# Biased copies of product 1, the order of t1's block sums, and sums moved between engines in a two-layer graph kernel

## The chip, the cores and the metric

The kernel runs on one core of one Trainium2 chip, in float32. The metric is the time of one execution on the device in microseconds (us). Six runs of the kernel before took 1493.88 to 1495.98 us, with a median of 1494.96.

Engines are named as the profile names them: PE is TensorE (matmuls), PEld its weight loads, DVE is VectorE, ACT is ScalarE, POOL is GpSimd, SP is SyncE, which issues most of the transfers.

## The reference

`x` has 128 batches of 128 nodes and 512 features. Cut to what is computed (`b` has one value per node; `Wq`, `Wk`, `Wv` are 512x512 with 512 biases each):

```
h = max(layernorm(x), 0)                       # layer 0, per batch
A = adj @ h;  C = adj @ h + b
x = x + max over n of relu(A + (C - A))        # one value per node, added to all features
h = max(layernorm(x), 0)                       # layer 1
q, k, v = h @ Wq + bq, h @ Wk + bk, h @ Wv + bv   # 8 heads of 64
w = softmax(q k^T / 8 + mask(adj == 0))
x = x + w v
```

Layer 0 adds the same amount to every feature of a node, which the second layernorm takes away again. So one normalised `h` serves both layers.

## The kernel before, in words

The 128 batches are worked in 32 groups of four. The order of every engine's instructions is the order in which the program writes them (`manual_schedule`); nothing is reordered by a planner. The engines run side by side and wait for one another by semaphores where one needs what another made, or overwrites what another still reads.

**Before a group.** `norm(m)` (line 269) makes the statistics of batch m on DVE, then two tiny operations on POOL (a power, line 289, and a product, line 291); `norm_end(m)` (307) then makes `hn` on ACT and, unless told otherwise, adds the bias of v to `x` on POOL with `add_bv` (312, 128x512). Inside the loop ACT and POOL do the statistics (`norm_act`, 293). `adjacency(m)` (356) is one matmul with a maximum on DVE behind it, both through one PSUM bank. `blocks(m)` (316) transposes `hn` in 32x32 blocks on DVE, and `move(m)` (325) puts the blocks of two batches in place with 16 transfers from SP; the result is `hT`.

**The projections.** `Products` (442) makes q, k or v of a group by a scheme of seven half-size products instead of eight, on sums of quarters of the weights (`s1` to `s4`, `weight_sum`, 424) and of `hT` (`t1` to `t4`, `h_sum`, 373). Products 1 and 6 are plain matmuls (line 481). Products 2, 3, 4, 5 and 7 are made by the same scheme once more, on 128x128 blocks (line 587), each from seven block products: `first` (two of them), `inner` (three), `sixth` and `seventh`. For these, block sums of the quarters of `h` are made on POOL (`h_blocks`, 381, tiles `h`) and block sums of the weights once at the start (`weight_blocks`, 409, four sums of 128x128 for each of five quarters, line 422). `h_blocks(g, k, parts)` has k = 0 to 4 for t4, b22, b21, t1 and t3, and the parts 0 (128x256, read by `first`), 1 (128x128, read by `sixth`, `seventh`) and 2 (128x128, `t[:, 3]`, the last, read by the third matmul of `inner`). `h_blocks(g, 3, (2,))`, the last block sum of t1, is read by inner(5). In the text (3,2) means k = 3, part 2.

Results are collected in a tile `u` with three parts and a tile `t` (T7). Product 1 is copied by ACT to `u[0]` (line 508), and for q and k again to `u[1]` with the second half of the bias (two activations, line 496; for v a plain copy, line 510). Then, in the order of `steps` (699), for product p of group g:

- step 0: what is left of the projection before (`end3`), then p1 (matmuls and the copies)
- step 1: first(5), added by DVE to u[0] (first_to, 639); first(7), copied by ACT to T7 (675, 676); product 6 in between; sixth and seventh of 5 and 7, each followed by its addition; `end6`: u[2] = product 6 + bias + u[0] (`add_pf`, line 521, two instructions; for v one, line 517)
- step 2: first(2), seventh(7), terms7(0): u[0] += T7 on POOL (690, 128x512); for q four `h_blocks` on POOL (`mid`); inner(2), inner(5), first43 (first of 4 and of 3), first_to(4) on DVE (665), inner(7); for v `h_sum` of t3 for the next group on POOL (379); terms7(1): u[1] += T7 on POOL
- step 3: `end7`: u[0] = product 7's bank + bias + u[0] (`add_pf`), `end5` (527)
- steps 4 and 5: sixth and seventh of 2, 4 and 3 with their additions (sixth_to(4) is on DVE, line 665, and adds to u[1] and u[2]), inner of 4 and 3, `end4`, and in the next projection `end3`.

A matmul that adds to a bank waits until the addition that reads this bank is through: seventh(4) for sixth_to(4), sixth(7) for first_to(7), inner(4) for `end7`, inner(3) for `end5`.

**A period of the loop** (line 894) is `apply` of the group before (786), `scores` of this group (756, then exponentials on ACT, 764), v of this group, q and k of the next. A table `todo` puts other work behind each step: the masks on POOL (768, four of them behind steps 2 and 3 of q and four behind step 2 of k), block sums, norms, loads. The masks must be done before `apply` reads the weights. The list of h_blocks behind v's last step is line 945. Group 0's first projections (lines 844 to 893) are made without the block scheme for k, by plain q for q.

Of the kernel before, what the change touches and what calls it, by code (L numbers as in the profile page):

```python
# [45 lines left out]
F32 = mybir.dt.float32  # L46
# [6 lines left out]
P = 128  # L53
G = 4
# [115 lines left out]
def tile_adj_preln_d2(  # L170
# [33 lines left out]
    adjT = const.tile([P, D], F32, name="adjT")  # L204
    live = const.tile([P, D], F32, name="live")
    RS = const.tile([P, B, H], F32, name="RS")
    ones = const.tile([P, 1], F32, name="ones")
    flag = const.tile([1, 1], I32, name="flag")
    V = const.tile([P, G, H, HE], F32, name="v")
# [3 lines left out]
    def fast(ctx):  # L213
# [98 lines left out]
        def add_bv(m):  # L312
            x_m = x_of(m)
            nc.gpsimd.tensor_tensor(x_m, x_m, bv_sb, op=ALU.add)  # L314
# [123 lines left out]
        def weight_sums(eng, n):  # L438
            for k in range(4):
                weight_sum(eng, n, k)  # L440

        class Products:
# [59 lines left out]
                nc.vector.tensor_tensor(to, to, what, op=ALU.add)  # L502

            def p1(self):
                self.a = self.bank(0)
                self.mm(self.a, "a11", "b11", True)
                self.u = U
                nc.scalar.copy(self.u[:, 0], self.a)  # L508
                if self.n == "v":
                    nc.scalar.copy(self.u[:, 1], self.a)  # L510
                else:
                    self.biased(self.u[:, 1], self.a, 1)

            def add_pf(self, out, bank, f):

                if self.n == "v":
                    nc.vector.tensor_tensor(out, bank, self.u[:, 0], op=ALU.add)
                    return
                bias = bq_sb if self.n == "q" else bk_sb
                for r in range(2):  # L520
                    nc.vector.scalar_tensor_tensor(
                        out[:, r], bank[:, r], bias[:, 2 * f + r : 2 * f + r + 1],
                        self.u[:, 0, r], op0=ALU.add, op1=ALU.add,
                    )

            def add(self, out, bank, more):
# [172 lines left out]
        def steps(p, tail, mid, t2, t3, late):  # L699

            t = tail + [lambda: None] * 8
            return [
                [t[0], p.p1],
                [call(p.first, 5, True), call(p.first_to, 5), t[1], call(p.p6a, (0,)),
                 call(p.first, 7, True), call(p.first_to, 7), call(p.p6a, (1, 2)),
                 call(p.sixth, 5), call(p.sixth_to, 5), call(p.sixth, 7), call(p.sixth_to, 7),
                 call(p.p6a, (3,)), call(p.seventh, 5), call(p.seventh_to, 5), p.end6],
                [call(p.first, 2, True), call(p.seventh, 7), call(p.seventh_to, 7), call(p.terms7, 0), mid,
                 call(p.inner, 2), p.end2] + [call(p.inner, 5), call(p.first43)][::-1 if late else 1] +
                [call(p.first_to, 2), call(p.first_to, 4),  # L710
                 call(p.inner, 7), t3, call(p.terms7, 1)],
                [p.end7, p.end5],
                [call(p.sixth, 2), call(p.sixth_to, 2), call(p.sixth, 4), call(p.sixth, 3), call(p.sixth_to, 4)],
                [call(p.inner, 4), call(p.inner, 3), call(p.seventh, 2), call(p.seventh, 4),
                 call(p.seventh, 3), call(p.seventh_to, 2), call(p.seventh_to, 4)] + ([t2, p.end4] if p.n == "v" else [p.end4]),
            ]
# [4 lines left out]
        def call(m, *a):  # L721
            return lambda: m(*a)
# [119 lines left out]
        with tc.manual_schedule():  # L842
# [13 lines left out]
            transposes(3)  # L856
            for m in range(G):
                add_bv(m)
            weight_sums(nc.gpsimd, "v")
            plain_q(0, 0)  # L860
            weight_sums(nc.vector, "k")
            for k in range(4):
# [7 lines left out]
            adjacency(3)  # L870
            plain_q(1, 0)
            blocks(G)
            weight_blocks(nc.vector, "v", (3, 2, 0))
            blocks(G + 1)
            move(G + 1)
            weight_blocks(nc.vector, "v", (1, 4))
            plain_q(1, 1)
            k = Products(0, "k")
            more = {
                0: [(adjacency, G), (norm, G + 2), (norm_end, G + 2)],  # L880
                1: [(norm, G + 3), (norm_end, G + 3), (blocks, G + 2)],
                2: [(adjacency, G + 1)], 3: [(blocks, G + 3), (move, G + 3)],
                4: [(adjacency, G + 2)], 5: [(adjacency, G + 3)],
            }
            for s, p in enumerate((k.p1, k.p6, k.p2, k.p7, k.p5, k.p4, k.p3)):
                p()
                for f, m in more.get(s, ()):
                    f(m)
                if s < 2:
                    add_bv(G + s)  # L890
                elif s < 6:
                    weight_sum(nc.gpsimd, "q", s - 2)
            weight_blocks(nc.gpsimd, "q", (3, 2))
            for g in range(NG):
                b = g * G
                if g > 0:
                    apply(g - 1)
                scores(g)
                part, tail = [], []
                for p in [Products(g, "v")] + [Products(g + 1, n) for n in "qk" if g + 1 < NG]:  # L900
                    if p.n == "v" and g in (0, NG - 1):
                        part += [
                            [p.p1], [p.p6], [p.p2], [p.p7], [p.p5], [p.p4, p.p3],
                        ]
                        continue
                    t2 = t3 = mid = lambda: None
                    if p.n == "v":
                        t2 = lambda: h_sum(g + 1, 2)
                        t3 = lambda: h_sum(g + 1, 0, nc.gpsimd)
                    if p.n == "q":  # L910
                        mid = lambda: [
                            h_blocks(g + 1, k, (i,)) for k, i in ((0, 1), (1, 1), (0, 2), (1, 2))
                        ]
                    part += steps(p, tail, mid, t2, t3, g == NG - 2)
                    tail = later(p)
                    if p.n == "k":
                        part[-1] += tail
                        tail = []
                todo = {s: [] for s in range(len(part))}

                def add(s, *what):
                    todo[s].append(what)

                m = b + 2 * G
                if g + 1 < NG:
                    if g > 0:
                        for i in range(G):
                            residual(b - G + i, nc.gpsimd)
                    if m < B:
                        norm(m)  # L930
                        norm(m + 1)
                    else:
                        count(0, b)
                    if 0 < g < NG - 1:
                        add(0, adjacency, m - 1)
                    if g == 0:
                        add(3, h_sum, 1, 0)
                    add(4, h_sum, g + 1, 1)
                    if g == 0:
                        add(4, h_sum, 1, 2)  # L940
                    for k, i in ((4, 0), (4, 1), (3, 0), (3, 1)):
                        add(4, h_blocks, g + 1, k, (i,))
                    add(5, h_blocks, g + 1, 2)
                    add(5, h_sum, g + 1, 3, nc.gpsimd)
                    for k, i in ((0, 0), (1, 0), (3, 2), (4, 2)):
                        add(5, h_blocks, g + 1, k, (i,))
                    if g + 2 < NG:
                        for s, l in next_norms(m).items():
                            for what in l:
                                add(s, *what)  # L950
                    for k, s in enumerate((8, 8, 9, 9, 14, 14, 14, 14)):
                        add(s, mask, nc.gpsimd, b + k // 2, k % 2)
                    if g + 2 < NG:
                        add(0, load, 2 * g + 5)
                    if g + 3 < NG:
                        add(8, load, 2 * g + 6)
                else:
                    for k, s in enumerate((0, 0, 0, 0, 2, 2, 3, 4)):
                        add(s, mask, nc.vector, b + k // 2, k % 2)
                    for i, s in enumerate((0, 0, 0, 1)):  # L960
                        add(s, residual, b - G + i)
                for i in range(G):
                    add((2, 5, 9, 15)[i] if g + 1 < NG else i + 1, add_c, b + i)
                if g == 0:
                    add(0, weight_blocks, nc.gpsimd, "q", (0, 1, 4))
                    for s, k in ((0, 3), (0, 2), (1, 0), (1, 1), (3, 4)):
                        add(s, weight_blocks, nc.vector, "k", (k,))
                for s, ps_ in enumerate(part):
                    for p in ps_:
                        p()  # L970
                    for f, *args in todo[s]:
                        f(*args)
# [49 lines left out]
```

## Time and profile before

| | |
|---|---|
| median of 6 runs | 1494.96 us (1493.88 to 1495.98) |
| profiled execution, its own time | 1495.62 us |
| its span from first to last instruction | 1493.9 us |
| mean granted TensorE clock | 0.999 |
| PE / PEld / DVE / ACT / POOL busy | 99 / 90 / 79 / 44 / 88% |
| from the start to the first scores | 47.60 us |
| one period of the loop | 45.76 us |

The busy time of PE is the time in which a matmul was under way. A busy PE is not PE at its peak, since matmuls are pipelined: a lost tenth of a microsecond shows best in the weight loads, which in the block products follow each other every 0.11 us as long as nothing holds them. In a row of the timeline stand the start and the length in us, engine, line, operation, the tiles (output <- inputs), the shape, how many instructions were merged into the row, and in brackets the idle time ahead of it with what ended it. Every block product is two weight loads and two matmuls in the trace.

### The profile page before, as it was taken

To read this page: it belongs to the slowest core of one execution; us is meant where nothing else is said; L and a number is where in the kernel's file an instruction comes from. 1 tells how busy PE (TensorE), PEld (TensorE's weight loads), DVE (VectorE), ACT (ScalarE), POOL (GpSimd) and SP (SyncE) were. 2 spreads that over 40 slices of the span, in tenths; PEclk is the share of its full clock that TensorE was granted. 3 is DMA by queue.
4 is the path that set the end of the run, shared out by engine and by line. 5 is a ranking of instruction groups with operands and counts; after the bars stand their busy time and mean duration, and the time that the engine had idled before them with its cause. 6 is when DMAs were issued, how large, how long until landed. Compare 5 with 4: busy or idle time off the path is not lost.

```text
span 1493.9 us, 38616 instructions
## 1 busy us (share of the span) xinstructions
PE 1474.0 (99%) x14565; PEld 1343.4 (90%) x14565; DVE 1186.0 (79%) x2984; ACT 661.9 (44%) x1487; POOL 1318.5 (88%) x1564
## 2 busy tenths in 40 slices
PE   7999999999999999999999999999999999999997
PEld 5899999999999999999999999999999999999997
DVE  7787877778877878778787778887787877778877
ACT  3444454454444444544444444435444444444432
POOL 5989889889899898898898988989989989889882
PEclk9999999999999999999999999999999999999999
DMA  5232222322223312233222233122332222331211
GB/s 168 53 86 42 63 77 77 86 65 46 76 75 84 86 33 72 76 78 86 58 52 76 76 85 86 28 77 75 80 86 56 54 74 76 86 84 28 62 43 59
DMA packets 307836, 105.67 MB, mean 71 GB/s; under 512 B 273152, under 2 KB 273280, under 8 KB 307648
## 3 DMA queue, kind: packets, MB, share of 16 engines
q1 hardware_dynamic: 307328, 102.84, 26.7%
q8 instruction: 117, 1.92, 0.6%
q14 instruction: 71, 0.58, 0.1%
q0 software_dynamic: 176, 0.27, 0.1%
q10 hardware_dynamic: 144, 0.07, 0.0%
HBM read 37.03 MB, written 33.55 MB: 47 GB/s over the span
## 4 chain that ended last, share of the span: by engine, by line
PE 77%; POOL 19%; DVE 2%; issue 1%; DMA 1%; ACT 0%; SPq 0%; DVEq 0%; POOLq 0%
PE bk L587 37%; PE bk L481 17%; POOL h L396 13%; PE bk L786 8%; PE bk L756 8%; PE bk L348 7%; POOL u L690 3%; POOL hs L379 3%; DMA wk_sb<-in_L_gnn_Wk_dram 1%; DVE sk_sb L434 0%; DVE ssv_sb L422 0%; DVE hs L379 0%; POOL xp L314 0%; ACT hn L308 0%; DVE o L804 0%
## 5 line engine op out<-in xcount | busy, mean ns | idle before, releaser
L768 POOL TENSOR_TENSOR w<-w,live 128x512 f32<-128x512 f32 x248 | 308.7, 1279 | 0.0
L690 POOL TENSOR_TENSOR u<-u,t 128x512 f32<-128x512 f32 x184 | 234.5, 1275 | 76.2 <-DVE t L639 53.3
L665 DVE TENSOR_TENSOR u<-u,bk 128x256 f32<-128x256 f32 x552 | 206.2, 414 | 58.5 <-PE bk L587 35.7
L764 ACT ACTIVATE w<-bk 128x512 f32<-128x512 f32 x256 | 128.9, 624 | 271.1 <-PE bk L756 271.1
L639 DVE TENSOR_TENSOR u<-u,bk 128x128 f32<-128x128 f32 x368 | 109.2, 317 | 99.4 <-PE bk L587 96.4
L308 ACT ACTIVATE hn<-xp,nmr,rstd 128x512 f32<-128x512 f32 x124 | 100.5, 810 | 159.2 <-POOL nmr L305 97.3
L816 POOL TENSOR_TENSOR o<-xp,o 128x512 f32<-128x512 f32 x122 | 152.2, 1287 | 20.2 <-DVE RS L803 20.2
L314 POOL TENSOR_TENSOR xp<-xp,bv_sb 128x512 f32<-128x512 f32 x128 | 159.9, 1289 | 3.2 <-ACT hn L308 1.9
L352 DVE TENSOR_REDUCE amax<-bk 128x1 f32<-128x512 f32 x128 | 86.6, 677 | 75.0 <-PE bk L348 75.0
L508 ACT COPY u<-bk 128x512 f32<-128x512 f32 x95 | 55.1, 580 | 183.6 <-PE bk L481 183.6
L348 PE MATMUL bk<-hn,adjT 128*128 128x512 f32 x248 | 127.0, 594 | 0.9 <-DVE amax L352 0.9
L786 PE MATMUL bk<-v,w 128*64 128x65 f32 x4096 | 126.5, 222 | 0.0
L786 PEld LDWEIGHTS bk<-v,w 128*64 128x64 f32 x4096 | 122.0, 138 | 4.1 <-issue 0.3
L756 PE MATMUL bk<-qT,kT 64*128 64x128 f32 x2048 | 122.9, 275 | 0.0
L756 PEld LDWEIGHTS bk<-qT,kT 64*128 64x128 f32 x2048 | 116.8, 188 | 2.5 <-issue 0.3
L587 PE MATMUL bk<-ssv_sb,h 128*128 128x128 f32 x720 | 111.4, 277 | 0.1
L587 PEld LDWEIGHTS bk<-ssv_sb,h 128*128 128x128 f32 x720 | 98.6, 191 | 14.2 <-issue 13.9
L396 POOL TENSOR_TENSOR h<-hT,h 128x128 f32<-128x128 f32 x186 | 96.4, 518 | 7.3
L804 DVE TENSOR_TENSOR o<-bk,RS 128x448 f32<-128x448 f32 (+1 forms) x161 | 93.7, 582 | 5.5
L812 ACT ACTIVATE xp<-xp,c 128x512 f32<-128x512 f32 x128 | 91.2, 715 | 0.0
L587 PEld LDWEIGHTS bk<-h,ssq_sb 128*128 128x128 f32 x558 | 75.8, 191 | 15.3 <-DVE u L665 7.7
L321 DVE STREAM_TRANSPOSE tb<-hn 128x512 f32<-128x512 f32 x124 | 87.1, 703 | 2.2 <-ACT hn L308 2.2
(198 smaller groups left out, 4077.0 us busy)
## 6 DMA issues: line engine op xcount, KB each, us to landing
out_dram<-o SPq DMA_DIRECT2D x128, 256.0 KB, 2.4
xp<-in_x_dram SPq DMA_DIRECT2D x62, 512.0 KB, 5.0
hT<-tb SPq DMA_DIRECT2D x992, 32.0 KB, 1.9
xp<-in_x_dram SPq DMA_DIRECT2D x4, 256.0 KB, 3.9
wq_sb<-in_L_gnn_Wq_dram SPq DMA_DIRECT2D x2, 512.0 KB, 7.8
wk_sb<-in_L_gnn_Wk_dram SPq DMA_DIRECT2D x2, 512.0 KB, 10.0
wv_sb<-in_L_gnn_Wv_dram SPq DMA_DIRECT2D x2, 512.0 KB, 11.0
bv_sb<-in_L_gnn_bv_dram POOLq DMA_DIRECT2D x1, 256.0 KB, 7.8
```

The lines of the kernel that those rows point to most:

```text
L314: nc.gpsimd.tensor_tensor(x_m, x_m, bv_sb, op=ALU.add)
L348: nc.tensor.matmul(PA[m], adjT, HN[m], start=True, stop=True)
L396: nc.gpsimd.tensor_tensor(o, x, y, op=ALU.subtract)
L481: nc.tensor.matmul(bank[:, r, :], lhs, rhs, start=first and i == 0, stop=i == 3, skip_group_check=True,)
L587: nc.tensor.matmul(out, lhs, rhs, start=start, stop=True, skip_group_check=True)
L665: nc.vector.tensor_tensor(to, to, what, op=ALU.add)
L690: nc.gpsimd.tensor_tensor(u, u, T7, op=ALU.add)
L756: nc.tensor.matmul(psc[j][:, f, :], KT[g][r, f, i * D : (i + 1) * D], QT[g][r, f, i * D : (i + 1) * D], start=True, stop=True,)
L764: nc.scalar.activation(w[:, j], psc[j], AF.Exp, scale=HD ** -0.5)
L768: eng.tensor_tensor(w[:, j], w[:, j], live_h, op=ALU.mult)
L786: nc.tensor.matmul(pav[r, c : c + HE], w[:, h % 2, h // 2, r], V[:, i, h, :], start=True, stop=True,)
L816: eng.tensor_tensor(y, x_of(b), y, op=ALU.add)
```

## The change

The two versions compute the same. For q and k, u[0] is now product 1 with the second half of the bias, by two activations, as u[1] was already. `end7` needs no bias any more and is one addition of 128x512; `end6` adds the difference of the two halves of the bias, made once at the start (`DB`). u[1]'s copy is issued after first_to(7), in `steps`; before, it came right behind u[0]'s. The plain `p1` (v of the first and the last group, k of group 0) still makes both copies together.

Behind v's last step, (3,2) is issued before (1,0).

At the start, three of the five block sums of Wv's quarters (12 of 20 instructions) are issued on POOL, before norm(6); the other eight stay on DVE. The four add_bv of group 1 are issued together after norm(7).

```
+    db_sb = const.tile([P, 2, 2], F32, name="db_sb")
+    DB = {n: db_sb[:, i] for i, n in enumerate("qk")}
...
             def p1(self):
+                self.p1a()
+                self.copy(1)
+
+            def copy(self, k):
+                if self.n == "v":
+                    nc.scalar.copy(self.u[:, k], self.a)
+                else:
+                    self.biased(self.u[:, k], self.a, 1)
+
+            def p1a(self):
                 self.a = self.bank(0)
                 self.mm(self.a, "a11", "b11", True)
                 self.u = U
-                nc.scalar.copy(self.u[:, 0], self.a)
-                if self.n == "v":
-                    nc.scalar.copy(self.u[:, 1], self.a)
-                else:
-                    self.biased(self.u[:, 1], self.a, 1)
+                self.copy(0)
 
             def add_pf(self, out, bank, f):
-                if self.n == "v":
+                if self.n == "v" or f == 1:
                     nc.vector.tensor_tensor(out, bank, self.u[:, 0], op=ALU.add)
                     return
-                bias = bq_sb if self.n == "q" else bk_sb
                 for r in range(2):
                     nc.vector.scalar_tensor_tensor(
-                        out[:, r], bank[:, r], bias[:, 2 * f + r : 2 * f + r + 1],
-                        self.u[:, 0, r], op0=ALU.add, op1=ALU.add,
+                        out[:, r], bank[:, r], DB[self.n][:, r : r + 1], self.u[:, 0, r],
+                        op0=ALU.add, op1=ALU.add,
                     )
...
-                [t[0], p.p1],
+                [t[0], p.p1a],
...
-                 call(p.first, 7, True), call(p.first_to, 7), call(p.p6a, (1, 2)),
+                 call(p.first, 7, True), call(p.first_to, 7), call(p.copy, 1), call(p.p6a, (1, 2)),
...
             for m in range(G):
                 add_bv(m)
+            for n, b_sb in (("q", bq_sb), ("k", bk_sb)):
+                nc.gpsimd.tensor_tensor(DB[n], b_sb[:, 0:2], b_sb[:, 2:4], op=ALU.subtract)
             weight_sums(nc.gpsimd, "v")
...
-            weight_blocks(nc.vector, "v", (3, 2, 0))
+            weight_blocks(nc.vector, "v", (3, 2))
+            weight_blocks(nc.gpsimd, "v", (0, 1, 4))
             blocks(G + 1)
             move(G + 1)
-            weight_blocks(nc.vector, "v", (1, 4))
...
-                0: [(adjacency, G), (norm, G + 2), (norm_end, G + 2)],
-                1: [(norm, G + 3), (norm_end, G + 3), (blocks, G + 2)],
+                0: [(adjacency, G), (norm, G + 2), (norm_end, G + 2, False)],
+                1: [(norm, G + 3), (norm_end, G + 3, False), (blocks, G + 2)],
...
-                if s < 2:
-                    add_bv(G + s)
-                elif s < 6:
+                if s == 1:
+                    for m in range(G):
+                        add_bv(G + m)
+                elif 1 < s < 6:
                     weight_sum(nc.gpsimd, "q", s - 2)
...
-                    for k, i in ((0, 0), (1, 0), (3, 2), (4, 2)):
+                    for k, i in ((0, 0), (3, 2), (1, 0), (4, 2)):
```

More of the change, by code (lines that the diff above doesn't have):

```diff
@@ L886, in fast @@
                 p()
-                for f, m in more.get(s, ()):
-                    f(m)
-                if s < 2:
-                    add_bv(G + s)
-                elif s < 6:
+                for f, *args in more.get(s, ()):
+                    f(*args)
+                if s == 1:
+                    for m in range(G):
+                        add_bv(G + m)
+                elif 1 < s < 6:
                     weight_sum(nc.gpsimd, "q", s - 2)
```

## The prediction

> **What bounds the kernel now.** I read the page first (busy times, chain), then the waits, then the timeline of one period in the middle and of the head. The page:
>
> ```profile
> PE 1474.0 (99%) x14565; PEld 1343.4 (90%) x14565; DVE 1186.0 (79%) x2984; ACT 661.9 (44%) x1487; POOL 1318.5 (88%) x1564
> ...
> PE 77%; POOL 19%; DVE 2%; issue 1%; DMA 1%; ACT 0%; SPq 0%; DVEq 0%; POOLq 0%
> ```
>
> TensorE is busy throughout, yet POOL holds 19% of the chain that ended last. A period (apply to apply) takes 45.76 us, 30 times alike, so a wait of 0.1 us in it is worth 3 us. I look for every place where TensorE loses time, and for what releases it. The waits name one by POOL:
>
> ```profile
> PEld bk L587 <- POOL h L396: 7.7, 30, 0.3
> ```
>
> In the timeline this is inner(5) of q, which reads the last block sum of t1. The same window by engine (start, us, instruction):
>
> ```profile
> 701.07 1.28 POOL L379 TENSOR_TENSOR hs<-hT 128x512 f32<-128x512 f32 x1 [0.66 <-DMA out_dram<-o]
> ...
> 711.16 0.45 POOL L396 TENSOR_TENSOR h<-hT,h 128x128 f32<-128x128 f32 x1
> ...
> 711.66 0.30 PEld L587 LDWEIGHTS bk<-h,sq_sb 128*128 128x128 f32 x2 [0.25 <-POOL h L396]
> ...
> 714.88 1.27 POOL L690 TENSOR_TENSOR u<-u,t 128x512 f32<-128x512 f32 x1
> ...
> 716.18 0.42 DVE L665 TENSOR_TENSOR u<-u,bk 128x256 f32<-128x256 f32 x1 [0.31 <-POOL u L690]
> ```
>
> POOL's block sum ends at 711.61 and the weight load starts 0.05 later; its predecessor stood at 711.22 and loads follow each other by 0.11 here, so 0.33 us is lost. But the reader should follow POOL on: from 701.07 it runs without a pause through 20 instructions to 716.15, the end of terms7(1). DVE's sixth_to(4) waits for that, ends at 716.60, and seventh(4) on TensorE, which writes the bank that sixth_to(4) reads, loads at 716.65, 0.05 later. So seventh(4) too is held by POOL, by 0.03 us beyond the 0.11 pace. And POOL's run starts when TensorE's inner(7) of v has read t3, whose buffer line 379 overwrites (the row names a DMA; in 17 other periods it names TensorE).
>
> The head, until the first scores at 47.60, has TensorE waiting on DVE and ACT:
>
> ```profile
> 33.41 1.99 PE L481 MATMUL bk<-hT,wk_sb 128*128 128x256 f32 x8 [0.50 <-ACT u L496]
> ...
> 35.69 1.13 PE L348 MATMUL bk<-hn,adjT 128*128 128x512 f32 x2 [0.29 <-DVE amax L352]
> ...
> 37.94 1.99 PE L481 MATMUL bk<-hs,sk_sb 128*128 128x256 f32 x8 [1.11 <-DVE u L521]
> ...
> 44.84 1.10 PE L348 MATMUL bk<-hn,adjT 128*128 128x512 f32 x2 [0.60 <-DVE amax L352]
> ```
>
> **Part 1, the order of the block sums of t1.** POOL issues the same instructions; (3,2) moves ahead of (1,0), so it ends at about 710.91 (0.73 us of (1,0) earlier) and inner(5) has no wait. (1,0) ends at 711.61 instead of 711.16; its reader, first(3) in first43, loaded at about 712.5 and would load at about 712.2, so it is still in time. TensorE gains 0.33 us there. What is late next: seventh(4). POOL's 15.08 us from t3 to terms7(1) holds the same instructions, each start still fixed by the one before, and its start is fixed by TensorE's own inner(7) of v. So sixth_to(4) ends when it did, and TensorE waits there for all that it gained. I take 0. The ends: 0, and 0.33 x 30 = 10 us if the later wait gave way.
>
> **Part 2, product 7's term.** end7 for q and k is one addition of 128x512 instead of two instructions of 128x256. Rows: the pair took 0.87 (714.08 to 714.95), v's plain addition 0.69: 0.18 us earlier. Behind it in q and k, inner(4) waits for the bank that end7 reads and inner(3) for the one that end5 reads: loads at 715.00 and 715.73 come 0.03 and 0.06 late by the 0.11 pace (same in k). Both waits go. In q the time is again taken back at seventh(4): 0. In k, POOL's terms7(1) was released by DVE (0.71 us idle before it), so k is not held at seventh(4); there TensorE arrives 0.085 us earlier at the apply. But the masks stand next:
>
> ```profile
> 727.79 5.00 POOL L768 TENSOR_TENSOR w<-w,live 128x512 f32<-128x512 f32 x4
> ```
>
> They end at 732.79, started behind terms7(1), which this edit doesn't move. The apply starts at 729.60; the odd heads of its fourth element come 3.26 us later (seven eighths of 128 loads at the 0.029 pace), 732.86; with 0.05 from POOL to TensorE they could start at 732.84. So of 0.085 only about 0.02 is left: 0.4 us over 30 periods, ends 0 and 2.5. end6 keeps its two instructions and reads DB, ready long before: 0.
>
> **Part 3, the copies of product 1.** For q and k there are four activations instead of a copy and two: u0 comes from two (0.84 a pair) instead of one copy (0.57), 0.27 later; u1's pair now stands behind first_to(7). In k:
>
> ```profile
> 719.53 0.57 ACT L508 COPY u<-bk 128x512 f32<-128x512 f32 x1
> 720.00 0.84 ACT L496 ACTIVATE u<-bk,bk_sb 128x256 f32<-128x256 f32 x2
> 720.73 0.27 ACT L675 COPY t<-bk 128x128 f32<-128x128 f32 x1
> 720.87 0.40 ACT L676 COPY t<-bk 128x256 f32<-128x256 f32 x1
> ...
> 721.54 0.29 DVE L639 TENSOR_TENSOR u<-u,bk 128x128 f32<-128x128 f32 x1 [0.32 <-PE bk L587]
> ```
>
> L676 ends at 721.27 and sixth(7), which writes that bank, loads at 721.32, 0.09 later than its pace. With u1 behind, L676 ends by about 721.1 (its matmuls are then what it waits for): the 0.09 goes, and it lies before first43, so terms7(1) and the masks move along with it. 0.09 x 28 = 2.5 us. u0's delay: DVE's first_to(5) starts at 720.41 instead of 720.13, end3 of q behind it at 720.81, and sixth_to(5) can start at 721.42; it waits for TensorE until 721.54 anyway. Cover 0.12 us; were it gone, 3 us per 0.1. In q DVE is busy to 707.6, u0 comes at 707.4: nothing. In v the copies only change places before a wait for TensorE: nothing. u1 ends about 0.9 us later than before, over 3 us before first_to(4) adds to it.
>
> **Part 4, the head.** Twelve of DVE's 20 block sums of v's weights go to POOL, before norm(6). DVE's 20 with the transposition run from 29.73 to 34.95. Eight are left; beside POOL's own block sums such eight took 50.33 to 53.33 (0.375 each, against 0.23 alone). So DVE is through with them at 32.7, with the transposition at 33.4, 1.6 us earlier; the maximum and end6's pair follow, and product 7's matmuls start at about 36.4 instead of 37.94. There p2, 0.25 later by the extra copies (to 33.66), and the adjacency product become the limit. Gain 1.5. POOL's twelve at 0.51 (row of 50.35 to 54.43) run from 29.23 to 35.4; norm(6)'s power waits for DVE until 35.0 anyway, so hn(6) comes at about 37.1 instead of 38.49, before blocks(6) is up on DVE. Second: norm(7)'s power was queued behind two add_bv (38.57 to 41.02), and DVE then waited 1.95 us for hn(7) with a maximum behind it; TensorE's 0.77 us wait at 44.84 hung on that. All four add_bv now stand behind norm(7): the power comes at about 37.1, and the wait goes. Gain 0.75. POOL then has 4 x 1.25 of add_bv from about 37.9 and is 2.3 us ahead as well, so the weight sums of q behind it keep their distance. SP's 32 moves of hT go back to back from 33.23 to 55.1, start 0.2 later and land by about 57; DVE's first sum of them would come at 57.2: barely covered, at most 0.5 lost. The two small sums DB on POOL lie in its 0.38 us wait for the weights of v at 16.9. Head: 2.25; ends 1.0 (the 0.75, and 0.25 of the rest) and 2.6.
>
> A rule against this part: the Trainium skill, Perfetto Trace Analysis, "Optimizing Scalar/DVE Operations", says DVE and GpSimd share a read port, so shifting work between them might not help; if they simply took turns (0.28 and 0.46 per pair) DVE's eight would last 5.9 us and the gain of 1.5 would be a loss of about 1.3. The rows of 50.33 to 54.43 show 3.0 us for such eight, and I go by the rows.
>
> **Sum.** 2.25 (head) + 2.5 (k's copies) + 0.4 (k's end7) + 0.1 (first group) = 5.25 us. The profiled execution took 1495.62 (span 1493.9): 1490.4. The median of the runs shown is 0.66 below it: 1489.7.
>
> **Rivals.**
> A. POOL's run is not what holds q: then parts 1 and 2 give 0.33 + 0.09 more per period, 12 us: 1478. For it: the wait of 7.7 us by name. Against: the 0.05 us between POOL, DVE and TensorE at seventh(4).
> B. Only the head gains, or only k: another wait in k takes the 0.09 (sixth_to(5) has 0.12 in hand, the masks 0.02): 2 to 3 us, 1492.5.
> C. Slower: u0 from two activations holds first_to(5). The place is k, DVE at 720.13. It costs once the pair ends over 0.12 us later than its row says, 3.1 us for each 0.1 beyond; 0.08 beyond cancels the head's gain. If all 0.27 came through to seventh(5) in each k, it is 8.4 - 2.3: 1501. Against: 0.32 us of idle time before sixth_to(5).
> D. The head gives nothing, since POOL's twelve sums delay hn(6) (they would have to take 0.65 each, not 0.51), and B holds too: no change, 1495.
>
> **How the numbers follow.** Forecast 0.69 (1488 to 1492), A 0.08, B 0.12, C 0.05, D 0.06. Two in ten left out: from 1486.0, part way to A, to 1493.2, past B. About 0.2% (3 us) is what a measurement can tell from no change: below 1492.0 lie the forecast, A and a little of B: 0.77; within 0.2% the rest of B, D and a little of C: 0.18; slower 0.05.
>
> **What the changed profile would show.** The wait for POOL L396 is gone; instead seventh(4) of q waits about 0.4 us behind DVE L665, itself behind POOL L690; POOL from t3 to terms7(1) still takes 15.1 us. sixth(7) of k follows at its pace. The period is 45.66. The first scores start at about 45.4. Wrong would be: a shorter stretch from v's inner(7) to q's seventh(4) (A), DVE L639 in k ending the wait of seventh(5) (C), scores at 47 or later (D).

## The result, and the profile after

The changed kernel takes 1491.63 us (median; 1490.08 to 1492.77), the kernel before, measured beside it, 1494.89 (1493.64 to 1496.30): a ratio of 0.9977, 95% interval 0.9971 to 0.9984, or 3.3 us less. The forecast was 1489.7, 5.25 us less, with a range of 1486.0 to 1493.2. So direction and range hold, and the size is 2 us too large. The profiled execution took 1490.91, 4.7 us less than the one of before; but the one lies 0.7 us below the median of its kernel and the other 0.7 above, so this pair doesn't settle the missing 2 us.

On the page, the busy time and the chain that ended last by engine:

```profile
PE 1467.5 (99%) x14565; PEld 1335.8 (90%) x14565; DVE 1168.8 (78%) x2909; ACT 679.2 (46%) x1550; POOL 1325.3 (89%) x1578
...
PE 68%; POOL 27%; DVE 2%; DMA 1%; issue 1%; ACT 0%; DVEq 0%; POOLq 0%
```

The busy time says little. The chain says that POOL holds more of the end than before (27% against 19%), although POOL's wait by name is gone. The lines of the waits (what waited for what: us in total, times, longest) show where it went:

```profile
DVE u L674 <- POOL u L699: 38.3, 61, 1.0
...
PEld bk L596 <- DVE u L674: 26.3, 91, 0.6
```

DVE's sixth_to(4) now waits longer for POOL's terms7(1) (22.8 us before), and TensorE's weight loads wait longer for sixth_to(4) (15.2 us before, 62 times). In the timeline of the same period of the loop as was shown of before (its apply starts at 680.27; by engine, one after another):

```profile
697.56 1.28 POOL L381 TENSOR_TENSOR hs<-hT 128x512 f32<-128x512 f32 x1 [0.65 <-DMA out_dram<-o]
...
711.37 1.27 POOL L699 TENSOR_TENSOR u<-u,t 128x512 f32<-128x512 f32 x1
```

```profile
712.67 0.42 DVE L674 TENSOR_TENSOR u<-u,bk 128x256 f32<-128x256 f32 x1 [0.82 <-POOL u L699]
```

```profile
712.47 0.30 PEld L596 LDWEIGHTS bk<-h,ssq_sb 128*128 128x128 f32 x2
713.14 0.52 PEld L596 LDWEIGHTS bk<-h,ssq_sb 128*128 128x128 f32 x4 [0.37 <-DVE u L674]
```

POOL's run from t3 to the end of terms7(1) is 15.08 us, to the hundredth what it was. The loads ahead of seventh(4) stand at 712.47 and 712.58; the next should come at 712.69 and comes at 713.14: 0.45 us, where it was 0.03. All that inner(5), inner(4) and inner(3) gave back is there.

In k, ACT's copies are in the new order, and the four loads from 717.40 on stand 0.11 apart (before, four loads took 0.72 from 720.90, with the 0.09 us ahead of sixth(7) in it):

```profile
717.11 0.38 ACT L685 COPY t<-bk 128x256 f32<-128x256 f32 x1
717.37 0.85 ACT L498 ACTIVATE u<-bk,bk_sb 128x256 f32<-128x256 f32 x2
```

```profile
717.40 0.63 PEld L596 LDWEIGHTS bk<-h,wk_sb 128*128 128x128 f32 x4
```

The period is 45.65 us (45.76 before; forecast 45.66) in most cases, but 45.87 in the four that begin with the apply of groups 1, 9, 17 and 25. The first scores start at 44.96 (47.60 before; forecast 45.4):

```profile
33.43 1.99 PE L483 MATMUL bk<-hT,wk_sb 128*128 128x256 f32 x8 [0.46 <-ACT u L498]
35.26 1.02 PE L350 MATMUL bk<-hn,adjT 128*128 128x512 f32 x2
36.14 1.99 PE L483 MATMUL bk<-hs,sk_sb 128*128 128x256 f32 x8
...
42.28 1.02 PE L350 MATMUL bk<-hn,adjT 128*128 128x512 f32 x2
...
44.96 1.27 PE L765 MATMUL bk<-qT,kT 64*128 64x128 f32 x18
```

Product 7's matmuls start at 36.14 (37.94 before), and the fourth adjacency product no longer has its 0.60 us wait.

### The profile page after: what moved, and what is told of

It reads as the page before. It is cut to its first block, busy times and chain, and to the rows that moved or that the text cites. A ratio compares the mean times of both kernels' runs of the same rounds, so it can differ in the third digit from the quotient of the medians.

```text
span 1489.1 us, 38559 instructions
## 1 busy us (share of the span) xinstructions
PE 1467.5 (99%) x14565; PEld 1335.8 (90%) x14565; DVE 1168.8 (78%) x2909; ACT 679.2 (46%) x1550; POOL 1325.3 (89%) x1578
## 3 DMA queue, kind: packets, MB, share of 16 engines
q1 hardware_dynamic: 307328, 102.84, 27.4%
## 4 chain that ended last, share of the span: by engine, by line
PE 68%; POOL 27%; DVE 2%; DMA 1%; issue 1%; ACT 0%; DVEq 0%; POOLq 0%
PE bk L596 30%; POOL h L398 17%; PE bk L483 17%; PE bk L795 8%; PE bk L765 8%; POOL u L699 7%; PE bk L350 5%; POOL hs L381 2%; DVE u L674 1%; DMA wk_sb<-in_L_gnn_Wk_dram 1%; POOL ssq_sb L424 0%; DVE hs L381 0%; DVE sk_sb L436 0%; DMA adj_sb<-in_adj_dram 0%; POOL wq_sb L424 0%
## 5 line engine op out<-in xcount | busy, mean ns | idle before, releaser
L498 ACT ACTIVATE u<-bk,bq_sb 128x256 f32<-128x256 f32 x124 | 52.5, 479 | 158.8 <-PE bk L483 158.8
L596 PE MATMUL bk<-ssv_sb,h 128*128 128x128 f32 x720 | 111.5, 277 | 0.1
L596 PEld LDWEIGHTS bk<-ssv_sb,h 128*128 128x128 f32 x720 | 98.6, 191 | 14.2 <-issue 13.9
L398 POOL TENSOR_TENSOR h<-hT,h 128x128 f32<-128x128 f32 x186 | 96.5, 519 | 7.3
L596 PEld LDWEIGHTS bk<-h,ssq_sb 128*128 128x128 f32 x558 | 77.0, 191 | 26.4 <-DVE u L674 18.8
L596 PE MATMUL bk<-h,ssq_sb 128*128 128x128 f32 x558 | 91.0, 281 | 6.0 <-DVE u L674 5.9
L527 DVE TENSOR_TENSOR u<-bk,u 128x512 f32<-128x512 f32 x127 | 87.2, 687 | 5.2 <-PE bk L483 2.5
```

The lines of the kernel that those rows point to most:

```text
L398: nc.gpsimd.tensor_tensor(o, x, y, op=ALU.subtract)
L596: nc.tensor.matmul(out, lhs, rhs, start=start, stop=True, skip_group_check=True)
```

## The experiments

Twelve kernels ran. "Against before" is the difference of the medians with the kernel before measured in the same set. In the last column is the usual period of the loop in the profiled execution. From set to set the median of the kernel before moved between 1494.67 and 1495.55 us; where the text compares two of the other kernels by their medians, a difference of up to 0.9 us can come from that.

| kernel | edit | us | against before | ratio, 95% | period |
|---|---|---|---|---|---|
| changed | all of it | 1491.63 | -3.3 | 0.9971 to 0.9984 | 45.65 |
| e1_order | before + the order of t1's sums | 1494.75 | +0.1 | 0.9992 to 1.0010 | 45.76 |
| e2_head | before + the head's edit | 1493.65 | -1.0 | 0.9985 to 1.0003 | 45.76 |
| e3_copies | before + copies, DB, end7, end6 | 1491.76 | -2.9 | 0.9972 to 0.9990 | 45.64 |
| e6_u1_late | before + u[1]'s copy late | 1491.32 | -3.5 | 0.9966 to 0.9984 | 45.67 |
| e4_t3_on_dve | changed + (4,2) on DVE | 1479.52 | -15.2 | 0.9887 to 0.9917 | 45.28 |
| e5_order_old | e4 with the old order | 1488.29 | -6.6 | 0.9943 to 0.9971 | 45.52, 45.69 |
| e7_masks | changed + a mask moved | 1489.23 | -5.6 | 0.9950 to 0.9978 | 45.59 |
| e8_both | e4 + mask moved + (0,1) on DVE | 1493.84 | -1.0 | 0.9985 to 1.0003 | 45.76 |
| e9_best | e4 + mask moved | 1477.24 | -18.2 | 0.9874 to 0.9904 | 45.22 |
| e10_moves | changed + 4 early transfers on ACT | 1496.60 | +1.1 | 0.9999 to 1.0017 | 45.65 |
| e11_head_moves | e2 + 4 early transfers on ACT | 1499.96 | +4.5 | 1.0022 to 1.0049 | 45.76 |
| e12_moves_later | changed + 4 later transfers on ACT | 1490.32 | -5.2 | 0.9951 to 0.9978 | 45.67 |

### The parts one at a time: e1, e2, e3, e6

```
# e1_order, in the kernel before
-                    for k, i in ((0, 0), (1, 0), (3, 2), (4, 2)):
+                    for k, i in ((0, 0), (3, 2), (1, 0), (4, 2)):
```

> The kernel before with one edit: (3,2) ahead of (1,0). Theory P (POOL's unbroken run from t3 to terms7(1) holds q): the 0.33 us wait of inner(5) goes and seventh(4) of q waits about 0.35 us longer; the period stays at 45.76 us and the time within 0.5 us of the kernel before. Rival A (the wait that the profile names is what q loses): the period falls to 45.43 us and the time by about 10 us.

Measured 1494.75 beside 1494.67: no difference. The wait at inner(5) is gone and TensorE stands at seventh(4) for 0.37 us instead; the chain and the waits by name:

```profile
PEld bk L587 <- DVE u L665: 23.4, 91, 0.4
...
PE 67%; POOL 27%; DVE 3%; issue 1%; DMA 1%; ACT 0%; DVEq 0%; POOLq 0%
```

So the order alone is worth nothing in the kernel before, and rival A (10 us and more) falls.

```
# e2_head, in the kernel before
-            weight_blocks(nc.vector, "v", (3, 2, 0))
+            weight_blocks(nc.vector, "v", (3, 2))
+            weight_blocks(nc.gpsimd, "v", (0, 1, 4))
...
-            weight_blocks(nc.vector, "v", (1, 4))
...   # and the four add_bv of group 1 together after norm(7), as in the change
```

> The kernel before with the changes of the head alone (three block sums of Wv's quarters on POOL, four add_bv behind norm(7)). Theory: the first scores start at about 45.0 instead of 47.6 us, the period stays at 45.76, the time falls by 2.5 us. Rival D (POOL's twelve sums hold norm(6), or the gain of the head is lost behind it): scores at 47 or later, or the period longer, no change.

Measured -1.0 us, and the interval reaches no change. The trace has more: the first scores start at 44.52 and the first apply at 85.85, 3.1 us earlier than before, and the profiled execution took 1492.84, 2.8 us less than before's. The eleven runs lie between 1492.7 and 1495.2, no wider than the 27 of the kernel before beside them (1493.0 to 1496.5). So the head's gain stands in the trace, and in the median there is less of it; e10 to e12 ask why.

```
# e3_copies: the change without the new order and without the head's edit
```

> The kernel before with the changes to product 1's copies, end6 and end7 alone; order of block sums and head as before. Theory: sixth(7) of k no longer waits (0.09 us), inner(4) and inner(3) of q and k no longer wait (0.085), and of this only the 0.09 and 0.02 of k reach the end: period 45.65 us, time 3 us less; in q inner(5) still waits for POOL and seventh(4) takes the rest. Rival: all of it reaches the end, 0.09 + 2 x 0.085 = 0.26 a period, 8 us. Rival C (u0 from two activations holds first_to(5)): no gain, or up to 6 us more.

Measured -2.9, a period of 45.64: parts 2 and 3 as forecast (2.5 + 0.4). The wait at inner(5) stays ("PEld bk L596 <- POOL h L398", 7.2 us, 28 times).

```
# e6_u1_late, in the kernel before
             def p1(self):
+                self.p1a()
+                self.copy1()
+
+            def p1a(self):
                 self.a = self.bank(0)
                 self.mm(self.a, "a11", "b11", True)
                 self.u = U
                 nc.scalar.copy(self.u[:, 0], self.a)
+
+            def copy1(self):
                 if self.n == "v":
...
-                [t[0], p.p1],
+                [t[0], p.p1a],
...
-                 call(p.first, 7, True), call(p.first_to, 7), call(p.p6a, (1, 2)),
+                 call(p.first, 7, True), call(p.first_to, 7), p.copy1, call(p.p6a, (1, 2)),
```

> The kernel before with one edit: u1's copy of product 1 behind first_to(7) in the blocked projections; u0 stays a plain copy, end6 and end7 as before. Theory: this alone removes the 0.09 us wait of sixth(7) in k: period 45.67 us, time 2.5 us less. Rival (the gain of the copies came from end7 being one addition): no change.

Measured -3.5, at a period shorter by 0.09. Where u[1]'s copy stands is the whole of part 3; that u[0] takes a bias, and so two activations, is not needed for it. What e3 has above e6 in its period is 0.03, the size of end7's part.

### What holds q: e4, e5

If POOL's run sets seventh(4), one instruction less in it must show. (4,2), the last block sum of t3, goes to DVE, where there is room behind terms7(0).

```
# e4_t3_on_dve, in the changed kernel
-        def h_blocks(g, k, parts=range(3)):
+        def h_blocks(g, k, parts=range(3), eng=nc.gpsimd):
...
-                nc.gpsimd.tensor_tensor(o, x, y, op=ALU.subtract)
+                eng.tensor_tensor(o, x, y, op=ALU.subtract)
...
-                        mid = lambda: [
+                        mid = lambda: [h_blocks(g + 1, 4, (2,), nc.vector)] + [
...
-                    for k, i in ((0, 0), (3, 2), (1, 0), (4, 2)):
+                    for k, i in ((0, 0), (3, 2), (1, 0)):
```

> The changed kernel with one more edit: (4,2), one 128x128 subtraction of POOL's run, is made by DVE behind seventh_to(7) of q, where DVE was idle for 0.45 us. Theory P: POOL's run is 0.41 us shorter, seventh(4) of q waits 0.03 us instead of 0.44, and the period falls from 45.65 to about 45.25 us: 12 us less than the changed kernel, near 1479.5. Rival (something other than POOL's run holds q, for instance DVE's own queue): less than 3 us.

Measured 1479.52, 12.1 us below the changed kernel, as expected. The instruction took 0.46 on POOL; it takes 0.59 on DVE, and nobody waits for it there. The waits and the chain:

```profile
PEld bk L596 <- DVE u L674: 14.9, 62, 0.3
...
PE 94%; POOL 3%; DVE 1%; DMA 1%; issue 0%; ACT 0%; DVEq 0%; SPq 0%; POOLq 0%
```

POOL's part of the chain falls from 27% to 3%. This shows that POOL's run is what took the gain of parts 1 and 2 in q.

```
# e5_order_old, in e4
-                    for k, i in ((0, 0), (3, 2), (1, 0)):
+                    for k, i in ((0, 0), (1, 0), (3, 2)):
```

> The kernel of e4_t3_on_dve with the old order of the block sums, (1,0) ahead of (3,2). Theory P: once POOL's run no longer holds seventh(4), the order counts: inner(5) loses its 0.33 us again, seventh(4) no longer waits (0.085), and the period rises from 45.28 to about 45.52 us, 7 us in all, near 1487. Rival (the order is worth nothing anywhere): 1479.5.

Measured 1488.29, 8.8 us above e4, where 7 were expected. The wait that the change removed is back, by name:

```profile
PEld bk L596 <- POOL h L398: 9.1, 28, 0.4
```

Of the 29 like periods, 16 take 45.52 us, as expected; the other 13 take 45.69, which makes 2.2 us. In all of them but one, DVE's subtraction starts within 0.03 us of POOL's block sum (3,2), which inner(5) waits for. In the 16, DVE's takes 0.4 to 0.6 us and POOL's 0.45; in the 13, DVE's takes 0.28 and POOL's 0.61. One of the 13 (POOL, then DVE):

```profile
341.52 0.61 POOL L398 TENSOR_TENSOR h<-hT,h 128x128 f32<-128x128 f32 x1
```

```profile
341.53 0.28 DVE L398 TENSOR_TENSOR h<-hs,h 128x128 f32<-128x128 f32 x1
```

So the swap of two lines is worth nothing in the kernel before (0.1 us, within the noise) and, by the periods, 7 us once POOL's run is shorter; the rest of the 8.8 is this meeting of two engines.

### What holds k: e7, and the best version

```
# e7_masks, in the changed kernel: the fifth mask behind step 3 of q instead of step 2 of k
-                    for k, s in enumerate((8, 8, 9, 9, 14, 14, 14, 14)):
+                    for k, s in enumerate((8, 8, 9, 9, 9, 14, 14, 14)):
```

> The changed kernel with one mask moved from behind step 2 of k to behind step 3 of q, where POOL has idle time after it. Theory: in the changed kernel the masks hold the fourth element of the apply and take 0.065 to 0.085 us of what end7 gained in k; without that the period falls from 45.65 to about 45.58 us, 2 to 2.5 us less. Rival (the masks hold nothing): no change.

Measured 2.4 us below the changed kernel. In the changed kernel the 128 weight loads of an apply take 3.88 us, 3.81 before and 3.81 here. First the changed kernel, its masks and the apply beside them:

```profile
724.21 4.99 POOL L777 TENSOR_TENSOR w<-w,live 128x512 f32<-128x512 f32 x4
```

```profile
725.91 3.88 PEld L795 LDWEIGHTS bk<-v,w 128*64 128x64 f32 x128
```

and e7 (the masks' view, then the loads'):

```profile
723.40 3.74 POOL L777 TENSOR_TENSOR w<-w,live 128x512 f32<-128x512 f32 x3
```

```profile
725.11 3.81 PEld L795 LDWEIGHTS bk<-v,w 128*64 128x64 f32 x128
```

The masks end at 729.20 in the changed kernel, where the odd heads of the fourth element are due at 725.91 + 3.26 = 729.17: the apply waits 0.07 inside itself. So the masks do hold k's end, as Part 2 had it.

```
# e8_both, in e7 with e4's edit
-                        mid = lambda: [h_blocks(g + 1, 4, (2,), nc.vector)] + [
-                            h_blocks(g + 1, k, (i,)) for k, i in ((0, 1), (1, 1), (0, 2), (1, 2))
+                        mid = lambda: [h_blocks(g + 1, k, (i,), nc.vector) for k, i in ((4, 2), (0, 1))] + [
+                            h_blocks(g + 1, k, (i,)) for k, i in ((1, 1), (0, 2), (1, 2))
```

> The kernel of e4_t3_on_dve with (0,1) on DVE too and the mask moved as in e7_masks. Theory: POOL's run is another 0.41 us shorter, the 0.085 us that seventh(4) of q still waits there goes, the masks give 0.065: the period falls from 45.28 to about 45.13 us, near 1475. Rival (DVE's queue in step 2 of q becomes the bound: first_to(4) comes late for sixth(4)): 1479 or more.

Measured 1493.84, 14 us worse than e4: the expectation of a further gain was wrong. DVE's second subtraction falls beside POOL's terms7(0), and takes 1.35 us, where one with POOL idle takes 0.28:

```profile
709.47 1.31 POOL L699 TENSOR_TENSOR u<-u,t 128x512 f32<-128x512 f32 x1
...
709.58 1.35 DVE L398 TENSOR_TENSOR h<-hs,h 128x128 f32<-128x128 f32 x1
```

DVE's additions behind it (first_to(2), first_to(4)) come late, TensorE waits for them, and POOL's terms7(1) itself now waits 0.45 us for DVE:

```profile
712.53 1.27 POOL L699 TENSOR_TENSOR u<-u,t 128x512 f32<-128x512 f32 x1 [0.45 <-DVE u L674]
```

e9_best is e4 with e7's line, that is, e8 without DVE's second subtraction.

> The changed kernel with the block sum (4,2) on DVE behind terms7(0) of q, and with one of the four masks of k's step 2 moved to q's step 3 (five masks in q, three in k). The two edits gained 12.1 and 2.4 us one at a time. Theory: they touch two waits, seventh(4) of q behind POOL's run and the apply behind the masks of k, so the gains add: 1491.6 - 12.1 - 2.4 = 1477 us, a period of 45.20 us. Rival: the mask more in q now stands in POOL's way, since POOL's run and q's masks share one queue, and nothing or less than nothing is left of the 2.4: 1479.5 us or more, a period of 45.28 or more.

Measured 1477.24, a ratio of 0.9889 (0.9874 to 0.9904): the two gains add. It is the best of these kernels, 18.2 us below the kernel before. The chain is nearly TensorE's alone:

```profile
PE 95%; POOL 2%; DVE 1%; DMA 1%; ACT 0%; issue 0%; DVEq 0%; POOLq 0%
```

### Where the head's gain goes: e10, e11, e12

In the changed kernel, SP issues the 32 transfers of hT without a pause, and DVE's first sum of group 1 (line 381) waits for them. Behind it in DVE's order stand four sums of weights and v's end5 (line 536), which reads the bank that TensorE's product 3 of v adds to; that product's loads start at 60.22. First SP, then DVE, then TensorE's loads:

```profile
33.73 21.06 SPq L333 DMA_DIRECT2D hT<-tb  x32
```

```profile
57.05 0.86 DVE L381 TENSOR_TENSOR hs<-hT 128x512 f32<-128x512 f32 x1 [0.35 <-DMA hT<-tb]
...
59.42 0.68 DVE L536 TENSOR_TENSOR v<-bk,u 128x512 f32<-128x512 f32 x1
```

```profile
58.11 1.70 PEld L483 LDWEIGHTS bk<-wv_sb,hs 128*128 128x128 f32 x8
60.22 1.59 PEld L483 LDWEIGHTS bk<-sv_sb,hT 128*128 128x128 f32 x8 [0.41 <-POOL sq_sb L424]
```

The load comes 0.12 us after the end of end5 (60.10), and in e2, e5, e7 and e9 it comes 0.11 or 0.12 after it too: DVE releases it and not POOL, which the row names. Counted from the first scores it stands at 15.26 us, in the kernel before at 14.99 (62.59 - 47.60) and in e2 at 14.98 (59.50 - 44.52): 0.27 us is lost. In the profiled executions of e5, e7 and e8, which have the same head, it stands at 16.00 to 16.01, so 1.0 us is lost there; e4 and e9 have it at 15.26 too. (The expectations below put the two losses at 0.2 and 0.95.) The transfers are not the whole of it: in e5, DVE's first sum has no idle time ahead of it, and the load is late all the same (DVE, then the load):

```profile
56.71 0.87 DVE L381 TENSOR_TENSOR hs<-hT 128x512 f32<-128x512 f32 x1
```

```profile
60.16 1.59 PEld L483 LDWEIGHTS bk<-sv_sb,hT 128*128 128x128 f32 x8 [1.15 <-POOL h L398]
```

There, DVE's eight sums of weights ahead of it took 3.74 us (52.37 to 56.11) beside POOL's, against 2.86 in the changed kernel (53.16 to 56.02). That is rival N of the expectation below, in that execution.

```
# e10_moves, in the changed kernel; e11_head_moves is the same edit in e2
-                        nc.sync.dma_start(
+                        eng = nc.scalar if m == G + 1 and a == 0 else nc.sync
+                        eng.dma_start(
```

> The changed kernel with 4 of the head's 32 transfers of hT (those of the first 32 rows, for the first two batches of group 1) issued by ACT in place of SP. SP's 32 issues run from 33.73 to 54.8 in the changed kernel without a pause, 0.66 each; ACT is idle from 33.4 to 36.3. Theory M: SP's queue holds h_sum of group 1 on DVE (0.35 us of idle time at 56.7) and TensorE's stall at 60.2. With 28 issues SP is through at about 52.2, the idle time goes and with it the stall: 0.2 to 0.7 us less than the changed kernel, 1491.0 to 1491.4 us. Rival N: the sums of the weights on DVE and POOL hold that place, not the transfers: the stall stays, 1491.6 us; if ACT's issues hold hn of the third batch, up to 0.5 us more.

> The kernel before with the head's edit alone and the same 4 transfers issued by ACT. The head alone gave -1.0 us as a median, although its profiled execution reached the first apply 3.1 us earlier. Theory M: in part of the executions SP's queue of 32 transfers takes back what the head gained; with 28 on it the gain stands in all: 1492.0 to 1492.4 us, 2.3 to 2.7 below the kernel before. Rival N: the spread of the head's runs comes from elsewhere (when the weights and x arrive, say): 1493.6 us again.

Measured 1496.60 and 1499.96, 5.0 us above the changed kernel and 6.3 above e2: neither theory had that. I had looked at ACT's idle time in the trace (33.4 to 36.3), not at its order of instructions. The transfers wait for DVE's transposition, which ends at 33.5, and in ACT's order the copies of plain q and of product 1 stand behind them; in the changed kernel they ran at 31.1 to 33.4. ACT's queue is blocked until 36.2, and TensorE with it (ACT's instructions in e10, then the weight loads):

```profile
33.49 2.70 ACTq L334 DMA_DIRECT2D hT<-tb  x4
36.23 0.84 ACT L749 ACTIVATE qT<-bk,bq_sb 128x256 f32<-128x256 f32 x2 [5.29 <-DMA hT<-tb]
```

```profile
38.58 3.06 PEld L484 LDWEIGHTS bk<-hT,wk_sb 128*128 128x128 f32 x8 [5.34 <-ACT u L499]
```

```
# e12_moves_later, in the changed kernel
-                        nc.sync.dma_start(
+                        eng = nc.scalar if m == G + 3 and a == 0 else nc.sync
+                        eng.dma_start(
```

> The changed kernel with 4 of the head's 32 transfers of hT issued by ACT again, this time out of the second sixteen (the last two batches of group 1), where nothing of ACT's is behind them that is due soon: the fourth transposition ends at 39.68 in the changed kernel, ACT's copies of product 7 of k at 39.66, and its next instruction comes at 44.06. Theory M: the transfers hold h_sum of group 1 and through it TensorE at 60.2. SP's last issue then ends at about 52.2 in place of 54.8, DVE's sum has no idle time ahead of it (0.35 us in the changed kernel), TensorE's stall of 0.2 us at 60.2 (0.95 in other executions) is gone, and the stretch from the first scores to the first apply is 41.2 to 41.3 us in place of 41.44: 0.2 to 0.7 us less than the changed kernel, 1490.9 to 1491.4 us. Rival N: the stall hangs on the sums of the weights: the stretch stays at 41.44 or more, 1491.6 us.

Measured 1490.32 (1489.55 to 1490.67), 1.3 us below the changed kernel, more than expected, and 5.2 below the kernel before. Here the transfers are issued at 41.2 to 45.0 on ACT, and ACT's next instruction, at 45.03, is not due soon. SP is through at 52.74, DVE's sum has no idle time ahead of it, and the loads follow at their pace (SP, DVE, TensorE):

```profile
33.09 19.65 SPq L334 DMA_DIRECT2D hT<-tb  x28
```

```profile
55.98 0.87 DVE L382 TENSOR_TENSOR hs<-hT 128x512 f32<-128x512 f32 x1
```

```profile
57.47 1.70 PEld L484 LDWEIGHTS bk<-wv_sb,hs 128*128 128x128 f32 x8
59.20 1.70 PEld L484 LDWEIGHTS bk<-sv_sb,hT 128*128 128x128 f32 x8
```

So in the changed kernel SP's transfers cause this stall, by way of DVE. But it is not where the 1.3 us come from. The stretch from the first scores to the first apply is 41.33 us, against 41.44 in the changed kernel (42.18 in e5 and e7): of the 0.27 only 0.11 is left. Behind the stall, seventh(4) of q, which had no wait in the changed kernel here, comes 0.17 us late, since DVE's sixth_to(4) waits for POOL's run:

```profile
72.41 0.42 DVE L675 TENSOR_TENSOR u<-u,bk 128x256 f32<-128x256 f32 x1 [0.55 <-POOL u L700]
```

The two profiled executions differ by 1.4 us of their spans: in e12 the first scores come 0.64 earlier (0.53 of it already at product 1 of k, ahead of the edited transfers), the stretch is 0.11 shorter, the 31 periods together are 0.60 longer, and the end from the last apply on is 1.23 shorter, nearly all of it after the last busy instruction of any engine (5.2 us before the end in the changed kernel, 4.0 in e12). So the time that e12 gains beyond the 0.11 is not shown to come from the edit.

## Why the prediction came out right, and 2 us too large

**Part 1, the order: right.** Forecast 0, measured +0.1 (e1), which is within the noise. The step by which the time is taken back was as described: POOL's 15.08 us, sixth_to(4), seventh(4); e4 and e5 show it from both sides.

**Part 2, end7: right.** Forecast 0.4 for k and 0 for q. e3 measured parts 2 and 3 at 2.9 together, and e7 shows the masks hold the rest of it. The forecast let 0.02 of 0.085 through; with both gains of k in the period, the apply is held for 0.07 by the masks.

**Part 3, the copies: right.** Forecast 2.5; e6, which has only this, measured 3.5 as a median and 0.09 in the period, which over 29 periods is 2.6 (29 periods are alike in the kernel before, not 30). Rival C, u[0] later by two activations, has no trace: DVE's sixth_to(5) still waits for TensorE, by 0.43 us.

**Part 4, the head: right up to the first scores; what is left of it in the median is less than forecast.** The first scores came 2.64 us earlier for the forecast 2.25. DVE's eight sums took 3.56 us (29.52 to 33.08) for 3.0, POOL's twelve 5.78 (28.97 to 34.75) for 6.2, and hn(6) was there by 37.12, as forecast. In the eight profiled executions that have the head's edit and not e10's, the first scores stand at 44.16 to 44.96, in the four without it at 47.06 to 47.60. The step "barely covered, at most 0.5 lost" was right for the changed kernel (DVE's sum at 57.05 for 57.2, 0.27 lost) and too small for e5, e7 and e8 (1.0 lost), in e5 by DVE's sums beside POOL's and not by the transfers. As medians the head gave 1.0 us (e2 against before; by the interval of the ratio, between 2.2 gained and 0.4 lost) and 0.35 (the changed kernel's -3.26 against e3's -2.91), not 2.25. This is the term by which the sum is too large: 1.9 of the 2 us, with the 0.9 of the next paragraph in it. Where the untraced executions lose it stays open: in e2's traced one nothing is lost at 60.2, and the first apply comes 3.1 us earlier.

**What the sum didn't have.** The periods that begin with the apply of groups 1, 9, 17 and 25 are 0.22 us longer, 0.9 us in all. There, DVE's sum in v waits 0.31 us, for a load of `x` by the row, and comes to lie exactly beside POOL's block sum (4,1), which takes 1.00 us; first DVE and POOL in the period of group 1, then POOL in the next:

```profile
152.61 0.69 DVE L381 TENSOR_TENSOR hT<-hT 128x512 f32<-128x512 f32 x1 [0.31 <-DMA xp<-in_x_dram]
```

```profile
152.61 1.00 POOL L398 TENSOR_TENSOR h<-hs,h 128x128 f32<-128x128 f32 x1
```

```profile
198.47 0.78 POOL L398 TENSOR_TENSOR h<-hs,h 128x128 f32<-128x128 f32 x1
```

That is in POOL's run, so seventh(4) comes 0.22 later. e7, e10 and e12 have it in the same groups; the kernel before, e1, e2 and e3 don't, nor do e4 and e9, with a shorter run. Why this load matters only with all the parts together was not tried.

**On the profiled executions** the sum nearly closes: the first apply comes 2.5 us earlier, the 31 periods are 2.4 shorter (3.4 in e3, less the four long ones), the end 0.1 longer: 4.8 of the span. The sum's 0.1 for the first group was given without its working; e3 has 0.16 there (41.18 us from the first scores to the first apply, 41.34 before). Single executions of one kernel spread over 1.1 to 3.9 us here, before's too. Part of this may be when the first weights arrive, since product 1 of k starts between 27.4 and 29.2 in these traces, and the time behind the last busy instruction, 4.0 to 5.2 us; in the pair of before and changed both are nearly equal.

**The rule weighed in Part 4.** Taking turns would have made a loss of 1.3 us out of the sums moved to POOL; the first scores came 2.64 us earlier instead. The rows lie between: DVE's sums start 0.44 apart beside POOL's (0.23 in the trace of before, with POOL idle), POOL's 0.48 apart (0.41 in the loop). Here DVE is slowed to about POOL's pace, POOL by about a sixth.

## What to carry to other kernels

When a wait is removed, follow the releasing engine on to its next consumer: if its whole run is the limit, the wait only moves, and the same edit can be worth 0 now and 7 to 9 us after the run is cut by one instruction. Here POOL's fifth of the chain pointed at the run to cut. Before an issue is put on another queue, read that queue's order of instructions around it, not its idle time: a transfer that waits blocks all that is behind it.

## What the hardware showed that I had not expected

A DVE subtraction of 128x128 takes 0.28 us alone, 0.54 beside POOL's 128x128 ones, and 1.35 beside one of POOL's 128x512, which takes 1.31 (e8): it ends 0.15 us after POOL's. That fits a turn that is held for a whole instruction, and it makes a short DVE instruction's price depend on the length of what POOL does at that moment. Where both start within 0.03 us of each other (e5), one of the two keeps its own time and the other takes longer, DVE by 0.3 us or POOL by 0.15. The Trainium skill, SBUF — State Buffer, "SBUF: two separate sides", says just this of a DVE instruction with two SBUF inputs and a GpSimd instruction that reads SBUF: whichever starts first keeps the shared ports for its whole length. The rows of e8 agree.

After the 5.3 us in which TensorE stood still in e10, its clock was halved for the next 5 us; the windows view (us, then busy time and instructions by engine, granted clock, DMA share, GB/s) has it as 0.50:

```profile
38.50:43.20 4.70, 4.62 (x10) 3.39 (x11) 1.40 (x4) 2.35 (x5) 3.67 (x5) 0.50 0.31 50
```

Eight loads of the plain product take 3.06 us there, 1.59 in the changed kernel. So a wait of 5.3 us costs about 2 us more behind it: the first scores come 7.5 us later than in the changed kernel (52.50 and 44.96). The Trainium skill, TensorE: Matmul & The Clock Gate, "What's actually happening", states half rate after at least one idle window of about 3.4 us, and full rate after at least one busy window of the same length; both fit this run, with 5.3 us idle and 5 us of work at half rate.
